# Two graph layers with normalised residuals, 16 sequences on one core: the last tiles' order, the flag's place and the last root are changed

## The chip, the cores and the metric

The kernel runs on one core of one Trainium2 chip. A core has TensorE (PE, matrix products, with its weight loads as PEld), VectorE (DVE), ScalarE (ACT), GpSimd (POOL) and SyncE (SP), each with an instruction queue of its own, and DMA engines that move data between HBM and the on-chip memory. Engines wait for each other by semaphores. The metric is the device time of one execution in microseconds (us); lower is better.

## The reference, cut to what matters

There are 16 sequences of 1024 rows and 256 columns, each with an adjacency matrix of zeros and ones. Layer 0 adds to x a weighted sum of rows, and normalises each row. Layer 1 does so again with other weights:

```python
# layer 0, for adjacency of one kind
alpha = sigmoid(where(adj == 1, leaky((x * a0) @ x.T), -big))
x1 = layernorm(x + alpha @ x + bias)
# layer 1
H = x1 @ W;  s, d = H @ a_src, H @ a_dst
e = where(adj != 0, exp(-leaky(s[:, None] + d[None, :])), 0)
h = (e @ H) / e.sum(-1)
out = layernorm(x1 + elu(h))        # (v - mean) / sqrt(var + 1e-5)
```

The reference allows more kinds of adjacency. The kernel runs a fast pass for one kind and keeps a flag; if the flag says that the input or the numbers don't fit, a general pass (not run with these inputs) follows.

## The kernel before, in words

A sequence is cut into 8 tiles of 128 rows. `one_kind_pass` is a software pipeline written out by hand (`manual_schedule`: each engine takes its instructions in the order in which the program names them). In round b the scores of sequence b (layer 0), the sums of layer 1 of sequence b - 1 (`prev`) and the final scaling and storing of sequence b - 2 (`done`) stand side by side. Sequence 15 is the last. Behind the rounds only its layer 1 is left, and what remains of sequence 14. This stretch, called the end here, begins at L995, and it is what the change rewrites, with a little of the last round ahead of it.

What the steps are:

- `weights(b, m, t0, n)` (L651): VectorE makes the layer 1 weights e for 128 source rows m, here for half of the columns at a time.
- `sum1` (L661): one TensorE product of e with H, 257 columns (256 and the sum of the weights). Eight of them make one tile. `multiply1` (L1042) does the eight of one tile; the first four tiles are done together, one m after the other (L1018 to L1030); the last tile, number 7, is done in two halves of columns by `multiply_halves` (L1051).
- `elu(b, t, ...)` (L692): VectorE inverts the sum of the weights (L698, L699), ScalarE does Relu (L707) and Exp (L708) straight from the product. Tile 6 of the last sequence does the Relu on VectorE (L704, L705).
- `add(b, t)` (L710): VectorE joins both with x1 (L713, L720, for earlier sequences L715) and takes the row's moments (`stats`, L346 and L348). For earlier sequences `deviation1` (L364 on ScalarE) takes them.
- `center` (L388): GpSimd makes from the moments of several tiles the factor 1/sqrt(var + eps) by a power and one Newton step, and mean times factor (L356 to L394: eight small instructions).
- `scale1(b, t)` (L399): ScalarE normalises one tile, 256 columns; `scale0` does the same for x1. `store` (L733) issues a DMA of some tiles on SyncE's queue, in one case on ScalarE's.
- `end_half(c)` (L1072): all of the above for one half of tile 7, with moments into `st_end`.
- `root` and `invert_roots` (L998, L1004): the factors of tiles 6 and 7, with ScalarE's square root, VectorE's reciprocal and one Newton step, then two scalings on VectorE (L1129). The square root needs another function table on ScalarE, whose load shows as L1002.
- `total` (L1092): one small TensorE product sums the flags of 128 partitions; VectorE converts it (L1097), and `values_load` (L1104) has every engine read it into a register. The engines branch on it behind everything else; the last two tiles are stored in the branch that the flag selects (L1477), on SyncE.

In the end of the kernel before, the order is: first four tiles' products; then per tile t the products of tile t + 1 and `elu`, `add` of the tiles behind; the sum of the flag between the products of tiles 5 and 6; its conversion between the sums of tiles 4 and 5; its read on VectorE behind the sum of tile 5, on ScalarE ahead of the scalings of tiles 6 and 7 of sequence 14. GpSimd makes the factors of tiles 0 to 2, then of 3 to 5. PSUM tiles come from three pools, `ps_e`, `ps_t` and `ps_acc`.

## Time and profile before

| what | us |
|---|---|
| median of three runs | 1214.81 (1214.66 to 1215.09) |
| the profiled execution | 1214.68 |
| its span, first to last instruction | 1212.8 |
| VectorE busy | 1005.7 |
| ScalarE busy | 833.6 |
| GpSimd busy | 390.8 |
| last TensorE instruction ends | 1204.45 |
| last store issued (L1477) | 1208.80 |

The span is what the trace shows; the time of the execution lies 1.9 us above it. All starts below are us from the span's start. In the rows of a timeline the first number is the start, the second the duration, then engine, line, operation and what it writes and reads, and in brackets the idle time before it with what ended it. The granted TensorE clock is 0.998 of full speed in this execution.

### The profile page before, as it was taken

What the parts mean: (1) busy time and instruction counts of PE and PEld (TensorE: products, weight loads), DVE (VectorE), ACT (ScalarE), POOL (GpSimd) and SP (SyncE); (2) the same over time, 40 slices, a digit from 0 to 9 for tenths busy, and PEclk for the clock granted to TensorE, in tenths of its full rate; (3) what the DMA queues carried; (4) which work ended last, traced back from release to release, by engine and by line L of the source; (5) the groups of instructions that cost most, each with busy time, mean ns of one, the idle gap of its engine ahead of it and who ended that gap; (6) DMA issues with size and microseconds to landing.
All of it is one profiled execution on the core that took longest, in us unless ns stands there. A gap on an engine that the chain in (4) does not pass through costs nothing.

```text
span 1212.8 us, 16010 instructions
## 1 busy us (share of the span) xinstructions
PE 1203.4 (99%) x4373; PEld 819.0 (68%) x4373; DVE 1005.7 (83%) x1778; ACT 833.6 (69%) x2134; POOL 390.8 (32%) x716
## 2 busy tenths in 40 slices
PE   9999999999999999999999999999999999999997
PEld 7757657576675766758667586775757657576686
DVE  5798896988969789797897978979798897988956
ACT  4574767767677666875768757786676767767674
POOL 2310433504334142432414324143250433404343
PEclk9999999999999999999999999999999999999999
DMA  9768788697887878788697886978869688687412
GB/s 201 143 137 156 131 159 169 132 191 136 143 174 137 182 149 154 156 146 179 137 180 134 153 183 127 182 138 155 174 133 192 124 155 177 131 187 135 114 48 73
DMA packets 611609, 181.98 MB, mean 150 GB/s; under 512 B 488116, under 2 KB 593976, under 8 KB 611512
## 3 DMA queue, kind: packets, MB, share of 16 engines
q1 hardware_dynamic: 589328, 138.21, 57.0%
q0 software_dynamic: 20528, 41.95, 18.7%
q8 instruction: 37, 0.61, 0.2%
q10 hardware_dynamic: 1656, 0.72, 0.2%
q14 instruction: 60, 0.49, 0.2%
HBM read 153.09 MB, written 61.28 MB: 177 GB/s over the span
## 4 chain that ended last, share of the span: by engine, by line
PE 99%; DVE 0%; ACT 0%; issue 0%; ACTq 0%; DVEq 0%
PE acc L662 36%; PE pe L262 20%; PE pH L602 9%; PE pV L497 9%; PE pQ L497 8%; PE pW L497 8%; PE pR L497 4%; PE acc L416 2%; PE busy L149 0%; PE pxT L235 0%; PE pal L333 0%; ACT y L399 0%; ACT y_kept L399 0%; ACT L1002 0%; DVE y L713 0%
## 5 line engine op out<-in xcount | busy, mean ns | idle before, releaser
L662 PE MATMUL acc<-H,e 128*128 128x257 f32 x2032 | 446.9, 380 | 0.0
L662 PEld LDWEIGHTS acc<-H,e 128*128 128x128 f32 x2032 | 385.0, 190 | 69.0 <-issue 13.9
L262 PE MATMUL pe<-xa,xT 128*128 128x384 f32 (+1 forms) x720 | 249.2, 486 | 0.0
L262 PEld LDWEIGHTS pe<-xa,xT 128*128 128x128 f32 x720 | 133.9, 190 | 91.4 <-issue 52.9
L657 DVE SCALAR_TENSOR_TENSOR e<-p,pq_kept,adj 128x1024 f32<-128x1024 f32 (+1 forms) x136 | 159.9, 1229 | 0.1
L292 POOL TENSOR_TENSOR al<-ident,al 128x128 f32<-128x128 f32 x128 | 109.1, 865 | 140.6 <-DVE al L278 140.5
L475 DVE TENSOR_TENSOR al<-al 128x1024 f32<-128x1024 f32 (+2 forms) x105 | 143.8, 1369 | 5.1
L272 DVE TENSOR_TENSOR tb<-tb,low 128x384 f32<-128x384 f32 (+1 forms) x180 | 105.9, 596 | 46.2 <-ACT low L271 44.6
L130 ACT ACTIVATE junk<-adj,minus 128x2048 bf16<-128x2048 bf16 x64 | 127.3, 1990 | 0.1
L270 ACT ACTIVATE tb<-pe 128x384 f32<-128x384 f32 (+1 forms) x180 | 88.1, 489 | 56.1 <-PE pe L262 34.8
L104 POOL CAST adj<-x 128x1 bf16<-128x1 f32 x15 | 3.4, 223 | 352.4 <-DMA x<-y_rows 222.5
L602 PE MATMUL pH<-Wx,yT 128*128 128x258 f32 x480 | 114.1, 380 | 0.0
L497 PE MATMUL pV<-al,S 128*128 128x512 f32 x240 | 108.4, 593 | 0.0
L602 PEld LDWEIGHTS pH<-Wx,yT 128*128 128x128 f32 x480 | 91.1, 190 | 25.3 <-issue 6.7
L497 PE MATMUL pW<-al,x 128*128 128x512 f32 x240 | 107.9, 592 | 0.0
L497 PE MATMUL pQ<-al,x 128*128 128x512 f32 x240 | 107.9, 592 | 0.0
L325 DVE SCALAR_TENSOR_TENSOR al<-al,adj 128x512 f32<-128x512 f32 (+3 forms) x153 | 83.8, 564 | 17.5 <-DMA al<-mir 17.5
L707 ACT ACTIVATE h<-acc,rinv 128x256 f32<-128x256 f32 x81 | 38.1, 470 | 85.3 <-DVE rinv L699 75.7
L688 ACT ACTIVATE sums<-acc,tiny 128x1 f32<-128x1 f32 x45 | 11.8, 261 | 123.3 <-PE acc L662 123.3
L271 ACT ACTIVATE low<-pe 128x512 f32<-128x512 f32 (+1 forms) x192 | 94.9, 494 | 0.0
L278 DVE SCALAR_TENSOR_TENSOR al<-tb,adj 128x1024 f32<-128x1024 f32 (+3 forms) x120 | 90.9, 758 | 4.5
L399 ACT ACTIVATE y_kept<-y_kept,mr,r 128x256 f32<-128x256 f32 x120 | 64.9, 588 | 29.0 <-POOL mr L394 27.8
(152 smaller groups left out, 1661.6 us busy)
## 6 DMA issues: line engine op xcount, KB each, us to landing
adj<-in_adjT POOLq DMA_DIRECT2D x30, 1024.0 KB, 8.3
x<-in_x SPq DMA_DIRECT2D x15, 1024.0 KB
y_rows<-Z SPq DMA_DIRECT2D x240, 64.0 KB
x<-y_rows SPq DMA_DIRECT2D x30, 512.0 KB
out<-y_kept SPq DMA_DIRECT2D x30, 512.0 KB
xT<-in_x SPq DMA_DIRECT2D x112, 128.0 KB
p<-p_row POOLq DMA_DIRECT2D x15, 512.0 KB, 4.1
mir<-tb SPq DMA_DIRECT2D x60, 112.0 KB
```

What stands on the lines that cost most here:

```text
L130: nc.scalar.activation(junk, rows, AF.Square, bias=minus1, scale=2.0, accum_out=chk[:, b * CHECKS + n : b * CHECKS + n + 1],)
L262: nc.tensor.matmul(pe[:, 0:w], lhsT=xTs[b][:, c, ts(jt, P)], rhs=xas[b][:, c, ds(jt * P + o, w)], start=(c == 0), stop=(c == ND - 1),)
L270: nc.scalar.activation(tb[:, ds(o, w)], pe[:, 0:w], AF.Tanh, scale=0.5)
L271: nc.scalar.activation(low[:, 0:w], pe[:, 0:w], AF.Tanh, scale=0.5 * SLOPE)
L272: nc.vector.tensor_tensor(tb[:, ds(o, w)], tb[:, ds(o, w)], low[:, 0:w], ALU.max)
L278: nc.vector.scalar_tensor_tensor(als[b][:, jt, c0:c1], tbs[b, jt][:, c0 - jt * P : c1 - jt * P], 1.0, adjs[b, jt // HT][:, jt % HT, c0:c1] ...
L292: nc.gpsimd.tensor_tensor(diag, ident2, diag, ALU.add)
L475: nc.vector.tensor_tensor(out_, in0, in1, ALU.subtract)
L497: nc.tensor.matmul(banks[bank], lhsT=lhs[:, jt, :], rhs=rhs[:, jt, :], start=first and jt == 0, stop=jt == HT - 1, skip_group_check=True,)
L602: nc.tensor.matmul(pt, lhsT=x1Ts[b][:, c, ts(t, P)], rhs=Wx[:, c, :], start=(c == 0), stop=(c == ND - 1),)
L657: nc.vector.scalar_tensor_tensor(e, p_bcs[b][:, cols], q, rows, ALU.mult, ALU.min)
L662: nc.tensor.matmul(acc, lhsT=es[b][:, m, ts(t, P)], rhs=Hs[b][m], start=(m == 0), stop=(m == NT - 1),)
```

## The change

It touches the last round and the end alone.

- In the last round, the sum of tile 6 of sequence 14 moves ahead of the first four `weights`; the scalings of x1 for tiles 4 to 7 move from the last round into the end, behind the roots of sequence 14. These, with the sum of tile 7 and two deviations, move from step m = 4 to m = 3 of the first products, ahead of `weights` 6. A table set for ScalarE that holds both logarithm and exponential is named there.
- Four scalings of sequence 14 and their store move to right behind the first four tiles' products.
- The flag is summed behind the first four tiles; the products of tiles 4 to 6 are all named ahead of the first `elu`; the flag is converted behind the inverted sums of tiles 0 and 1, and read there, ahead of tile 0's sum.
- GpSimd makes the factors of tiles 0 to 3, of 4 and 5, and of 6 by itself. ScalarE scales two tiles ahead of tile 6's exponential and two behind it, then tile 4 between the halves, 5 behind them, and 6 behind the root. The stores are of tiles 0 to 3, and of 4 and 5, both on SyncE.
- Tile 7's factor is exp(-0.5 ln(var + eps)) on ScalarE with the same Newton step; there is no reciprocal, and VectorE scales tile 7 alone.
- The first half of tile 7 takes its PSUM tile from `ps_t`.

```diff
@@ add @@
-        full = (b, t) == (B - 1, NT - 2)
-        return stats(y, None if full else mv1s[b][:, t, :], f"1_{b}_{t}")
+        return stats(y, mv1s[b][:, t, :], f"1_{b}_{t}")
@@ the last round @@
             if last and t == 7:
+                add(prev, t - 1)
                 for m in range(4):
                     weights(b, m, 0, HT)
...
-            if t >= 1 and (last or t != 6):
+            if t >= 1 and t != (7 if last else 6):
                 add(prev, t - 1)
...
-            if last and t in (5, 7):
+            if last and t == 5:
                 for q in range(HT):
-                    scale0(b, (t - 5) // 2 * HT + q)
+                    scale0(b, q)
@@ the end @@
-    def root(t, st):
-        nc.vector.bn_aggr(mv1s[last][:, t, :], st)
-        r = roots_sb[:, t - (NT - 2) : t - (NT - 2) + 1]
-        nc.scalar.activation(r, mv1s[last][:, t, 1:2], AF.Sqrt, bias=eps)
-    def invert_roots():
-        v, r = mv1s[last][:, NT - 2 :, 1], roots_sb
-        nc.vector.reciprocal(r, r)
-        n = const.tile([P, 2], F32, tag="newton", name="newton")
+    def root():
+        mv = mv1s[last][:, NT - 1, :]
+        nc.vector.bn_aggr(mv, st_end)
+        v, r = mv[:, 1:2], const.tile([P, 1], F32, tag="root", name="root")
+        nc.scalar.activation(r, v, AF.Ln, bias=eps)
+        nc.scalar.activation(r, r, AF.Exp, scale=-0.5)
+        n = const.tile([P, 1], F32, tag="newton", name="newton")
...
     for m in range(NT):
-        if m in (3, 4):
-            weights(last, m + 3, 0, HT)
-        if m == 4:
+        if m == 3:
             add(done, NT - 1)
             for q in (NT - 2, NT - 1):
                 deviation1(done, q)
             r1s[done] = center(mv1s[done], f"1_{done}", unit=1.0 / D)
+            nc.scalar.preload_act_table_set("natural_log_exp_and_others")
+            for q in range(HT, NT):
+                scale0(last, q)
+        if m in (3, 4):
+            weights(last, m + 3, 0, HT)
...
+    for q in range(HT):
+        scale1(done, q)
+    store(done, 0, HT)
     check_pq(last)
...
-            acc = acc1(last, end, *((ps_e, "e") if c else (ps_acc, "acc")))
+            acc = acc1(last, end, *((ps_e, "e") if c else (ps_t, "t")))
...
-    for t in range(end):
-        if n_first - 1 <= t < end - 1:
-            multiply1(t + 1)
-        if t == 5:
-            multiply_halves()
-        if t == 4:
-            total = ps_t.tile([P, HT, P], F32, tag="t", name="total")[0:1, 0, 0:1]
-            nc.tensor.matmul(total, lhsT=any_bad, rhs=ones, start=True, stop=True)
+    total = ps_t.tile([P, HT, P], F32, tag="t", name="total")[0:1, 0, 0:1]
+    nc.tensor.matmul(total, lhsT=any_bad, rhs=ones, start=True, stop=True)
+    for t in range(n_first, end):
+        multiply1(t)
+    elu(last, 0, accs[0])
+    elu(last, 1, accs[1])
+    nc.vector.tensor_copy(flag, total)
+    multiply_halves()
+    n_bad = nc.values_load(
+        flag, min_val=0, max_val=P, skip_runtime_bounds_check_because="a number of partitions"
+    )
+    scale1(done, HT)
+    add(last, 0)
+    for t in range(2, end):
         elu(last, t, accs[t])
-        if 1 <= t < 6:
+        if t < 6:
             add(last, t - 1)
         if t == 5:
-            nc.vector.tensor_copy(flag, total)
             add(last, t)
         if t == 6:
-            st_full = add(last, t, invert)
-        if t in (4, 5):
-            r1s[last] += center(mv1s[last][:, ds(3 * t - 12, 3), :], f"1_{last}_{t}")
-        if t == 5:
-            n_bad = nc.values_load(
-                flag, min_val=0, max_val=P, skip_runtime_bounds_check_because="a number of partitions"
-            )
-        for q in range(2 * t - 4, 2 * t - 2) if 2 <= t < 6 else []:
+            add(last, t, invert)
+        for q in {2: (5, 6), 3: (7,)}.get(t, ()):
             scale1(done, q)
-            if q in (3, 7):
-                store(done, q - 3, HT)
-        if t == 5:
-            for q in range(3):
-                scale1(last, q)
-            store(last, 0, 3)
+        if t == 3:
+            store(done, HT, HT)
+        for t0, n in {4: [(0, 4)], 5: [(4, 2)], 6: [(6, 1)]}.get(t, []):
+            r1s[last] += center(mv1s[last][:, ds(t0, n), :], f"1_{last}_{t0}")
+        for q in {5: (0, 1), 6: (2, 3)}.get(t, ()):
+            scale1(last, q)
+    store(last, 0, HT)
...
     end_half(0)
-    scale1(last, 3)
     scale1(last, 4)
-    store(last, 3, 2)
     end_half(1)
-    root(end, st_end)
-    root(end - 1, st_full)
-    r = invert_roots()
     scale1(last, 5)
-    store(last, 5, 1, nc.scalar)
-    for q in (6, 7):
-        y = ys[last][q]
-        nc.vector.tensor_scalar(
-            y, y, mv1s[last][:, q, 0:1], r[:, q - 6 : q - 5], ALU.subtract, ALU.mult
-        )
+    store(last, 4, 2)
+    r = root()
+    scale1(last, NT - 2)
+    y = ys[last][end]
+    nc.vector.tensor_scalar(y, y, mv1s[last][:, end, 0:1], r, ALU.subtract, ALU.mult)
     return n_bad
```

More of the change, by code (lines that the diff above doesn't have):

```diff
@@ L1013, in invert_roots @@
         return r
-    roots_sb = const.tile([P, 2], F32, tag="root", name="root")
     n_first = 4
```

## The prediction, made before the result was known

> **What bounds the kernel now.** I read the page first: how long each engine is busy, and the chain that ended last.
>
> ```profile
> PE 1203.4 (99%) x4373; PEld 819.0 (68%) x4373; DVE 1005.7 (83%) x1778; ACT 833.6 (69%) x2134; POOL 390.8 (32%) x716
> ...
> PE 99%; DVE 0%; ACT 0%; issue 0%; ACTq 0%; DVEq 0%
> ```
>
> TensorE (PE) is busy for 99% of the span and carries 99% of the chain, so only two things can move the time: TensorE's work, which the change leaves as it is, and the few us in which TensorE no longer sets the end. Where those begin is told by the chain of waits, in order of time, from 1165 us on (start us, us, what).
>
> ```profile
> 1172.50 24.59 PE acc L662 x112
> ...
> 1199.59 1.09 ACT y_kept L399 x2
> 1200.68 1.18 ACT y L399 x3
> ...
> 1202.06 0.46 ACT y_last L708
> ...
> 1204.77 0.26 DVE h_end L1079
> ...
> 1205.44 0.98 ACT L1002
> ...
> 1206.73 0.49 ACT root L1002 x2
> ...
> 1208.36 0.41 DVE y_last L1129
> ```
>
> TensorE runs without a gap from 1172.50 to 1197.09. Then the chain leaves it: for one flag read and five scalings on ScalarE (L399), behind which tile 6's exponential (L708, 1202.06) stands, and from there over VectorE and ScalarE. The products end at 1204.45 (timeline), the last half tile's work starts on VectorE at 1204.68, the table load (L1002) and the two square roots hold the chain from 1205.44 to 1207.22, and the second of two scalings ends it at 1208.77. The timeline gives the single rows (start us, us, engine, line, operation).
>
> ```profile
> 1190.18 0.43 DVE L713 SCALAR_TENSOR_TENSOR y<-y,h 128x256 f32<-128x256 f32 x1 [0.53 <-ACT y L708]
> ...
> 1195.23 0.24 POOL L356 TENSOR_SCALAR ve<-mv 128x3 f32<-128x3 f32 x1 [7.30 <-DVE rinv L698]
> ...
> 1197.97 0.43 POOL L394 TENSOR_SCALAR mr<-mr 128x3 f32<-128x3 f32 x1
> ...
> 1200.93 0.16 DVE L698 TENSOR_SCALAR rinv<-acc 128x1 f32<-128x1 f32 x1 [0.47 <-PE acc L662]
> ...
> 1204.68 0.33 DVE L1079 TENSOR_SCALAR h_end<-acc,rinv_end 128x128 f32<-128x128 f32 x1
> ...
> 1205.44 1.28 ACT L1002 ACT_TABLE_LOAD   x1
> ```
>
> To be seen: tile 0's sum starts at 1190.18; the roots of three tiles on GpSimd (POOL) run from 1195.23 to 1198.40; tile 6's sum of weights is read at 1200.93, when its product has just ended; the table load lasts 1.28 us, and the root follows 0.01 us behind it. How long a read of the flag holds an engine's sequencer stands in the view of the tile flag:
>
> ```profile
> L1104 ACTq TENSOR_LOAD <-flag x1: 467/467/467, 1199.0 to 1199.0; - x1
> L1104 DVEq TENSOR_LOAD <-flag x1: 543/543/543, 1200.3 to 1200.3; - x1
> ...
> L1104 POOLq TENSOR_LOAD <-flag x1: 786/786/786, 1203.3 to 1203.3; - x1
> ```
>
> Last, SyncE's own waits: the final store is not held by its queue.
>
> ```profile
> SPq L1477 <- DVE y_last L1129: 2.9, 1, 2.9
> ```
>
> SyncE had been ready for 2.9 us when VectorE's last scaling released it at 1208.80. From there to the end of the span it is 4.0 us (transfer, branches, closing), which the change leaves alone. So I work out when that scaling ends, and compare with 1208.77.
>
> **Part 1: the order on VectorE ahead of the products.** Tile 6's sum of sequence 14 moves ahead of the first four weights. Its two instructions took 0.79 us (1177.12 to 1177.91), so the first weights go from 1174.24 to 1175.03 and, at 0.68 us, are there at 1175.71. TensorE takes 24.59 us for 112 products, 0.2196 us each, and its 16 products of the tile before end at 1176.01. Cover: 0.30 us; each later one of the weights has more, as TensorE needs 1.76 us per step and VectorE 0.68. If the cover is gone, the whole of it goes on the end. What is moved is the same work in total, so the checks of the flag are summed by 1187.92 as before, 2.2 us ahead of TensorE's end of the first four tiles, 1197.10 less 32 x 0.2196 = 1190.07; the sum of the flag on TensorE therefore doesn't stall it, and its place in the queue costs no more there than at 1197. I cost TensorE at 0.
>
> **Part 2: ScalarE between the products.** Four scalings of x1 (2.07 us) move from 1178.52 behind the deviations, with a table load ahead of them. Tile 7's sum now has two weights fewer ahead of it, 1.35 us, so its deviation ends about 1180.80 (before: 1182.15). Load 1.28 us: 1182.1; scalings: 1184.2; GpSimd's roots for sequence 14 took 5.7 us (1182.24 to 1187.93) and now end about 1186.6; four scalings of sequence 14 follow until 1188.8; tile 0's Relu is due at 1189.32. All of it lies in ScalarE's wait of 7.2 us ahead of that Relu, so it costs 0, with 0.5 us of cover; what is gone beyond it would still hide behind part 3 for 0.9 us. The store of these rows leaves SyncE about 1188.9, while no transfer runs.
>
> The Trainium skill, "ScalarE: Activation LUTs", section "What ACT_TABLE_LOAD costs", adds a drain of about 1.38 us to the load; the row shows none (the root starts 0.01 us after the load), and with a drain the load would still be hidden here, so the sum is the same by either.
>
> **Part 3: the flag ahead of tile 0's sum.** VectorE now converts the flag first. TensorE's sum of it ends about 1190.2, the conversion (0.12 us) at 1190.4, then VectorE reads the flag. That it holds the engine is seen on ScalarE, which went on 0.12 us after its own read. Bounds for VectorE's hold: 0 (it is the sequencer that loads) and 0.79 (POOL's row). I take VectorE's own row, 0.543, with 0.1 behind it: tile 0's sum starts at 1191.05 instead of 1190.18, **0.87 us later**. Waiting behind it on VectorE are the sums of all tiles. They follow at 1.70 us per tile (1191.67 to 1193.37), so tile 3's moments end at 1197.72 instead of 1196.85. The cadence catches up only where VectorE used to wait for products: tile 6's row at 1200.93 had 0.47 us idle ahead of it, and tile 4's 0.27. So tile 6's weights are still read at about 1200.93.
>
> The Trainium skill, "DMA: Bandwidth & Descriptors", section "Latency and other measured facts", has about 600 ns as the floor of a register load, which speaks against reading early; the rows here go down to 0.466 us, and by the page tile 0's sum would be 0.06 us later still.
>
> **Part 4: ScalarE ahead of tile 6's exponential.** The read and two scalings of sequence 14 leave this place. But two scalings of the last sequence stay ahead of the exponential, and they wait for GpSimd's roots of four tiles, which can't start before tile 3's moments: 1197.80. Four columns took 3.33 us (1160.68 to 1164.01) and 3.48 (1156.18 to 1159.66); I take 3.33: 1201.13. Scalings from 1201.25, exponential at 1202.25: **0.19 us later** than 1202.06. Two more scalings behind it push the last tile's Relu to 1203.60 (before 1203.35), so VectorE's chain for the halves is 0.25 us late: the second half starts at 1204.93, the last moments are there at 1206.57.
>
> **Part 5: the root.** No load now stands ahead of it, so the logarithm starts 0.1 us after the moments, at 1206.68 (the root of before: 1206.73). Logarithm and exponential of 128x1 have no row together; the nearest are the roots with the same operands, 0.278 and 0.294 us, and the dependent pairs of L612 and L613, 0.29 us from start to start. Ends: 0.48 for both (the two roots) and 0.94 (two of 256 columns, 0.47); I take 0.29 + 0.28: 1207.25. The reciprocal goes (0.195); three Newton steps of 0.195 each begin at 1207.29; the one scaling runs from 1207.88 to 1208.29, as tile 6's goes to ScalarE. That one needs GpSimd's root of one column, about 1206.7 by an estimate from the rows (2.05 us for 8 columns of the power, 1.04 for 4, 0.89 for 3), and ScalarE at 1207.2; it ends about 1207.75, beside the Newton steps, with 0.5 us of cover. Stores of tiles 4 and 5 leave at 1205.65 and take 0.75 us of transfer, clear of the last one.
>
> **Sum.** +0.25 (late halves), -0.30 (no wait for the load), +0.08 (logarithm and exponential against two roots), -0.19 (reciprocal), -0.33 (one scaling fewer; 1208.03 to 1208.36): -0.49, about **-0.5 us**. The profiled execution took 1214.68, a span of 1212.8 and 1.9 around it; it becomes 1214.2. The median of the runs shown, 1214.81, lies 0.13 above it, so I forecast 1214.3. About 0.2% (2.4 us) is what a measurement of this kernel can tell from no change; my sum is a fifth of that.
>
> **Rivals.**
> A, **the products set the end again**: if VectorE's hold is near 0, or GpSimd's roots of four are 0.75 us shorter, the exponential starts at 1201.39, right behind tile 6's weights. The second half then starts at 1204.50, as early as its product allows, and the last scaling ends at 1207.85: -0.9 us, 1213.9. For it: a load runs on the sequencer. Against it: ScalarE visibly stood still for its read. This is also the most that the change can give, since TensorE's end stays.
> B, **the read takes the place of the stall, and the kernel is slower**: every 0.1 us by which the flag delays tile 0's sum goes through tile 3's moments, GpSimd and ScalarE's two scalings to the end, one for one. It decides from a hold of about 1.0 us on (0.54 + 0.49); at 1.5 us it is +0.5, 1215.3. For it: the read waits for a value that the same engine wrote just before, of which no row exists, and POOL's row has 0.79. Against it: 1.0 is above all five rows of the read.
> C, **the first weights come late**: part 1's cover of 0.30 us is gone, TensorE stalls once, and all of it is paid: with 0.8 us of stall +0.3, 1215.1.
> D, **the change doesn't do what it says**: a second table load comes back ahead of the logarithm. The program of the changed kernel holds one load in this stage, so I give it no share.
>
> **How the numbers follow.** Forecast 0.61, A 0.14, B 0.10, C 0.08, a cause that I don't name 0.07. The range runs from A, with 0.5 below for the medians' scatter (1214.66 to 1215.09) and for unknown rows, to B at 1.5 us of hold: 1213.4 to 1215.4. Slower by over 0.2%: 0.02 of B, 0.01 of C, 0.02 unnamed, 0.05. Faster by over 0.2%: 0.03, unnamed alone, since A ends at -0.9. Within: 0.92.
>
> **What would show it.** Tile 0's sum near 1191.05 (part 3); the roots of tiles 0 to 3 on GpSimd ending near 1201.1 and ScalarE waiting for them (part 4); the products ending at 1204.45 as before, with no gap near 1176 and 1190 (part 1); the table load near 1181 inside ScalarE's wait (part 2); the logarithm 0.1 us behind the moments, one scaling of 0.41 us, the final store issued near 1208.3 (part 5). Wrong would be a gap on TensorE, ScalarE idle for more than 0.3 us behind the last moments, or a span that moves by over 1 us either way.

## The result and the profile after

| | before | after |
|---|---|---|
| median of 18 runs each, us | 1214.53 (1213.91 to 1215.09) | 1216.84 (1216.22 to 1218.30) |
| profiled execution, us | 1214.68 | 1216.43 |
| its span, us | 1212.8 | 1214.6 |

The ratio after to before is 1.002, with a 95% interval of 1.0012 to 1.0027. The changed kernel is 2.3 us slower; I had forecast 1214.3, about 0.5 us faster, with a range up to 1215.4. So both the sign and the range were wrong.

The page of the changed kernel, the same two lines as shown of before: busy time of TensorE first, then the chain by engine.

```profile
PE 1202.9 (99%) x4373; PEld 818.6 (67%) x4373; DVE 1005.2 (83%) x1776; ACT 834.4 (69%) x2135; POOL 394.0 (32%) x724
...
PE 96%; DVE 2%; DMA 1%; SPq 0%; ACT 0%; POOL 0%; issue 0%; DVEq 0%
```

TensorE is busy for the same time to 0.5 us, but the chain now leaves it earlier. The chain of waits of the changed kernel shows where (start us, us, what):

```profile
1172.21 17.62 PE acc L662 x80
...
1190.17 1.15 DVEq L1095
...
1191.42 0.44 DVE y L713
...
1201.27 0.25 POOL mr L394
...
1201.54 1.09 ACT y L399 x2
1202.63 0.37 ACT y_last L708
...
1206.61 0.22 DVE mv L1001
...
1206.86 0.30 ACT root L1003
...
1207.18 0.21 ACT root L1004
...
1208.00 0.41 DVE y_last L1127
```

It leaves TensorE at 1189.96, behind the sum of the flag (before: 1197.09). From there VectorE's sequencer (DVEq) holds it for 1.15 us with the read of the flag, then the sums of the tiles, GpSimd's roots of four (ending 1201.51), two scalings, tile 6's exponential. The last moments are there at 1206.82, logarithm and exponential follow, one scaling ends at 1208.41. In before that last scaling ended at 1208.77. By this view alone the changed kernel would be faster. The chain view ends with the last *counted* instruction, though: branches, semaphores and drains are not in it.

The view of the tile flag of the changed kernel (ns min/median/max, then first and last start):

```profile
L1095 ACTq TENSOR_LOAD <-flag x1: 1097/1097/1097, 1190.2 to 1190.2; - x1
...
L1095 DVEq TENSOR_LOAD <-flag x1: 1154/1154/1154, 1190.2 to 1190.2; - x1
L1095 PEldq TENSOR_LOAD <-flag x1: 492/492/492, 1202.0 to 1202.0; - x1
```

The read held VectorE for 1.154 us where I had taken 0.543. TensorE's read, 12 us later, took 0.492. The timeline of the changed kernel gives the rows that answer to those of before, and the stores:

```profile
1180.54 1.28 ACT L1020 ACT_TABLE_LOAD   x1
...
1181.84 2.08 ACT L399 ACTIVATE x<-x,mr,r 128x256 f32<-128x256 f32 x4
...
1189.21 7.55 SPq L734 DMA_DIRECT2D out<-y_kept  x2
...
1191.42 0.43 DVE L713 SCALAR_TENSOR_TENSOR y<-y,h 128x256 f32<-128x256 f32 x1 [1.29 <-ACT y L708]
...
1206.93 0.24 POOL L394 TENSOR_SCALAR mr<-mr 128x1 f32<-128x1 f32 x1
...
1208.50 0.37 SPq L1473 DMA_DIRECT2D out<-y_last  x1
```

Tile 0's sum stands at 1191.42. The table load lies near 1181 and the scalings follow 0.02 us behind it. The first half of sequence 14 is stored from 1189.21, 1.0 us ahead of the read. GpSimd's last instruction, tile 6's mean times factor, stands at 1206.93, and the final store is issued at 1208.50, 0.30 us earlier than in before.

So the work ends earlier and the span ends later: from the final store's issue to the span's end it is 6.1 us (1214.6 less 1208.50), in before 4.0. What lies there is seen in the instructions of the lines of the last branch. First the line of the branch, in the changed kernel (only GpSimd's sequencer, POOLq, is copied):

```profile
L1469 POOLq EVENT_SEMAPHORE  x5: 17/43/43, 1210.3 to 1210.7; - x5
...
L1469 POOLq COMPARE_BRANCH  x1: 45/45/45, 1206.9 to 1206.9; - x1
...
L1469 POOLq INC_SWDGE_SEM  x1: 732/732/732, 1210.8 to 1210.8; - x1
```

and the closing line behind it, also in the changed kernel:

```profile
L1507 POOLq EVENT_SEMAPHORE  x4: 17/17/17, 1213.8 to 1214.5; - x4
L1507 POOLq DRAIN  x3: 46/107/2273, 1211.5 to 1214.4; - x3
```

GpSimd's sequencer takes the branch at 1206.9, as it issues its last computing instruction. Its next instruction is at 1210.3: 3.4 us with nothing. Then come five semaphores, an INC_SWDGE_SEM of 0.73 us at 1210.8, and a DRAIN of 2.27 us from 1211.5 to 1213.8. 0.8 us later the program ends. What an engine does from its branch on is called its closing here. The same in the kernel before, the branch:

```profile
L1473 POOLq EVENT_SEMAPHORE  x5: 17/43/43, 1206.9 to 1207.2; - x5
...
L1473 POOLq COMPARE_BRANCH  x1: 45/45/45, 1204.2 to 1204.2; - x1
...
L1473 POOLq INC_SWDGE_SEM  x1: 732/732/732, 1207.3 to 1207.3; - x1
```

and its closing line:

```profile
L1511 POOLq EVENT_SEMAPHORE  x4: 17/17/17, 1212.0 to 1212.7; - x4
L1511 POOLq DRAIN  x3: 46/107/2273, 1208.0 to 1212.5; - x3
```

There the branch is at 1204.2, the long drain runs from 1208.0 to 1210.3, and GpSimd's next instruction is at 1212.0: GpSimd waited 1.7 us for the others, so its closing cost nothing. In the changed kernel the others wait for it. SyncE's waits in the changed kernel agree:

```profile
SPq L1507 <- DMA p_row<-pT: 2.0, 1, 2.0
...
SPq L1473 <- DVE y_last L1127: 1.1, 1, 1.1
```

SyncE stands 2.0 us for a semaphore of GpSimd's queue of DMAs (p_row<-pT was issued in the rounds; INC_SWDGE_SEM sets it at 1211.4), and had been ready 1.1 us before the final store could be issued.

My theory after this (C): GpSimd's factor of tile 6 moved its branch 2.7 us later (from 1204.2 to 1206.9), and a closing of 6 to 7 us behind it now sets the end. Two rivals: the read's hold makes it slower (R), or the order and size of the stores does (S).

### The profile page after: what moved, and what is told of

It reads as the page before. It is cut to its first block, busy times and chain, and to the rows that moved or that the text cites. A ratio compares the mean times of both kernels' runs of the same rounds, so it can differ in the third digit from the quotient of the medians.

```text
span 1214.6 us, 16018 instructions
## 1 busy us (share of the span) xinstructions
PE 1202.9 (99%) x4373; PEld 818.6 (67%) x4373; DVE 1005.2 (83%) x1776; ACT 834.4 (69%) x2135; POOL 394.0 (32%) x724
## 4 chain that ended last, share of the span: by engine, by line
PE 96%; DVE 2%; DMA 1%; SPq 0%; ACT 0%; POOL 0%; issue 0%; DVEq 0%
PE acc L662 36%; PE pe L262 20%; PE pH L602 9%; PE pW L497 8%; PE pV L497 8%; PE pQ L497 8%; PE pR L497 4%; PE acc L416 2%; DMA al<-mir 1%; SPq L302 0%; PE busy L149 0%; DMA mir<-tb 0%; PE pxT L235 0%; PE pal L333 0%; DVE al L278 0%
```

## The experiments

All times below are relative to the end of the products on TensorE, in the profiled execution of each kernel, so that kernels can be laid beside each other. "Drain" is the end of GpSimd's long DRAIN, "time" the median less that of before in the same session of runs (interval of the ratio).

| kernel | tile 0's sum | last moments end | final store issued | GpSimd's branch | drain | span end | time |
|---|---|---|---|---|---|---|---|
| before | -14.27 | 1.87 | 4.35 | -0.26 | 5.87 | 8.37 | |
| after | -12.74 | 2.66 | 4.34 | 2.73 | 9.64 | 10.48 | +2.31 (1.0012 to 1.0027) |
| e1 | -12.75 | 2.66 | 4.61 | -0.07 | 6.33 | 8.76 | +0.63 (0.9997 to 1.0015) |
| e2 | -14.26 | 1.84 | 4.32 | 0.34 | 6.58 | 8.47 | +0.05 (0.9991 to 1.0009) |
| e3 | -14.26 | 1.84 | 4.33 | 1.89 | 7.94 | 8.81 | +0.48 (0.9995 to 1.0013) |
| e4 | -14.26 | 1.88 | 4.36 | 3.69 | 10.15 | 10.98 | +2.54 (1.0011 to 1.0030) |
| e12 | -14.27 | 1.87 | 4.16 | 2.21 | 8.58 | 9.42 | +1.10 (0.9999 to 1.0017) |
| e5 | -13.35 | 2.08 | 4.03 | -0.66 | 5.72 | 8.39 | -0.10 (0.9994 to 1.0012) |
| e6 | -14.26 | 2.05 | 4.00 | -0.11 | 6.92 | 8.32 | +0.47 (0.9994 to 1.0012) |
| e9 | -14.26 | 1.87 | 3.86 | -0.25 | 5.88 | 8.43 | -0.25 (0.9989 to 1.0007) |
| e10 | -14.26 | 1.84 | 4.93 | -0.28 | 5.86 | 8.75 | +0.64 (0.9995 to 1.0013) |
| e11 | -14.26 | 1.84 | 3.74 | -0.31 | 6.02 | 8.37 | -0.46 (0.9986 to 1.0004) |
| e7 | -13.87 | 1.99 | 3.94 | -0.17 | 6.85 | 8.47 | +0.30, one run |
| e13 | -12.59 | 2.81 | 4.76 | 0.65 | 7.71 | 8.68 | +0.14, one run |
| e8 | -13.35 | 1.72 | 3.84 | -0.71 | 5.75 | 8.79 | -0.18 (0.9992 to 1.0010) |

**e1: tile 6's factor taken off GpSimd.** The changed kernel, with logarithm, exponential and Newton step over two columns, and VectorE scaling tiles 6 and 7. The read stays where the change put it.

```diff
-        v, r = mv[:, 1:2], const.tile([P, 1], F32, tag="root", name="root")
+        v, r = mv1s[last][:, NT - 2 :, 1], const.tile([P, 2], F32, tag="root", name="root")
...
-        for t0, n in {4: [(0, 4)], 5: [(4, 2)], 6: [(6, 1)]}.get(t, []):
+        for t0, n in {4: [(0, 4)], 5: [(4, 2)]}.get(t, []):
...
-    scale1(last, NT - 2)
-    y = ys[last][end]
-    nc.vector.tensor_scalar(y, y, mv1s[last][:, end, 0:1], r, ALU.subtract, ALU.mult)
+    for q in (6, 7):
+        y = ys[last][q]
+        nc.vector.tensor_scalar(
+            y, y, mv1s[last][:, q, 0:1], r[:, q - 6 : q - 5], ALU.subtract, ALU.mult
+        )
```

> The changed kernel, but tile 6's factor is made together with tile 7's by logarithm and exponential on two columns, and VectorE scales both; GpSimd makes no factor of tile 6. Theory C (closing): in the profile of the changed kernel GpSimd issues its branch at 1206.88, goes on at 1210.33, sets the semaphores of its DMA queue (0.73 us) and drains (2.27 us) until 1213.85, and the program ends 0.75 us behind that; in the kernel before its branch is at 1204.2, the drain ends at 1210.31 and GpSimd waits until 1212.03. So 7.0 us from GpSimd's last instruction to the end of its drain set the end. With its last factors made about 1204.4 the drain ends at 1211.2, the end is set by the last store again, one scaling (0.33 us) later than in the changed kernel: about 1.8 us faster than the changed kernel, within 0.3 us of the kernel before. Theory R (the flag's read, 1.15 us in front of tile 0's sum, is what was lost): no faster than the changed kernel, 2.3 us over the kernel before. Theory S (the last store lands late behind the larger stores on its queue): as R.

Measured 1215.15 beside 1214.52. Everything up to the last moments is as in the changed kernel, to 0.01 us; the final store even leaves 0.27 us later; and the kernel is 1.7 us faster than the changed one (+0.63 against +2.31, from two sessions whose kernel before has the same median, 1214.52 and 1214.53; nine of its eleven runs lie below the fastest of the changed kernel's, 1216.22). The branch line of this kernel:

```profile
L1470 POOLq EVENT_SEMAPHORE  x5: 17/43/43, 1207.2 to 1207.6; - x5
...
L1470 POOLq COMPARE_BRANCH  x1: 45/45/45, 1204.3 to 1204.3; - x1
...
L1470 POOLq INC_SWDGE_SEM  x1: 732/732/732, 1207.6 to 1207.6; - x1
```

The branch is 2.6 us earlier than in the changed kernel (1204.3 against 1206.9), and the closing lies in cover again. Theory C stands; the read and the stores, which are the same in both, can't be the main cause.

**e2, e3, e4: a dose on the kernel before.** Nothing of the change, only a copy of 128x1 on GpSimd whose result nobody reads, waiting for the first half's moments, for tile 7's moments, or for the inverted roots. One line, in three places (where the tile `late` is made is left out):

```diff
     end_half(1)
+    nc.gpsimd.tensor_copy(late, st_end[:, 0, 1:2])            # e2
     root(end, st_end)
+    nc.gpsimd.tensor_copy(late, mv1s[last][:, end, 0:1])      # e3
     root(end - 1, st_full)
     r = invert_roots()
+    nc.gpsimd.tensor_copy(late, r[:, 0:1])                    # e4
```

> The kernel before with one more copy of 128x1 on GpSimd that nothing reads, released by the moments of tile 7's first half, about 1204.9. Theory C: GpSimd's branch at about 1204.9, its drain ends at 1211.9, just short of 1212.03 when the others are ready: 0 to +0.2 us. Theories R and S: 0.

> The kernel before with the same copy, released by tile 7's moments, about 1206.4. Theory C: branch at 1206.5, drain until 1213.5, +1.4 us over the kernel before, though nothing waits for the copy. Theories R and S: 0.

> The kernel before with the same copy, released by the finished roots, about 1208.0. Theory C: branch at 1208.1, drain until 1215.1, +3.1 us over the kernel before. Theories R and S: 0.

Measured 1214.57, 1215.00 and 1217.06 beside 1214.52. The final store is issued within 0.03 us of that of before in all three. An idle copy of 0.35 us therefore costs 2.5 us if it is placed late enough. The branch line of e4, and behind it its closing line:

```profile
L1475 POOLq EVENT_SEMAPHORE  x5: 17/42/43, 1212.5 to 1212.8; - x5
...
L1475 POOLq COMPARE_BRANCH  x1: 45/45/45, 1209.5 to 1209.5; - x1
```

```profile
L1513 POOLq EVENT_SEMAPHORE  x4: 17/17/17, 1216.0 to 1216.7; - x4
L1513 POOLq DRAIN  x3: 46/107/2273, 1213.7 to 1216.5; - x3
```

e3 and e4 cost less than expected (+0.48 for +1.4, +2.54 for +3.1): the next instruction came 2.6 and 3.0 us behind the branch, and the closing took 6.05 and 6.46 us in place of the 7.0 I had allowed. Over all runs, branch to end of the drain took 6.05 to 7.06 us, of which the step from the branch to the next instruction is the part that varies (2.6 to 3.6).

**e12: tile 6's factor alone, on the kernel before.** GpSimd makes it, ScalarE scales the tile; the square root, the flag and the order stay.

```diff
-            st_full = add(last, t, invert)
+            add(last, t, invert)
+            r1s[last] += center(mv1s[last][:, ds(t, 1), :], f"1_{last}_{t}")
...
-    root(end - 1, st_full)
...
-    for q in (6, 7):
-        y = ys[last][q]
-        nc.vector.tensor_scalar(
-            y, y, mv1s[last][:, q, 0:1], r[:, q - 6 : q - 5], ALU.subtract, ALU.mult
-        )
+    scale1(last, end - 1)
+    y = ys[last][end]
+    nc.vector.tensor_scalar(y, y, mv1s[last][:, end, 0:1], r, ALU.subtract, ALU.mult)
```

> The kernel before with one part of the change alone: tile 6's factor on GpSimd by itself and its scaling on ScalarE; tile 7's by square root as before. Theory C: GpSimd has its flag read until 1204.1, then eight instructions of one column (2.4 us), so its branch comes about 1206.6, 2.1 us behind the products' end; 6.1 to 7.0 us to the end of its drain and 0.8 from there: +0.5 to +1.5 us against the kernel before, although VectorE's last scaling goes and the last store is issued 0.3 us earlier. Theory R (the flag's read is what was lost): 0.3 us faster, as the flag is read where it was.

Measured 1215.70 beside 1214.60, +1.10, though the store is issued 0.19 us earlier. The closing line of this kernel:

```profile
L1508 POOLq EVENT_SEMAPHORE  x4: 17/17/17, 1213.7 to 1214.4; - x4
L1508 POOLq DRAIN  x3: 46/107/2273, 1211.4 to 1214.2; - x3
```

The drain ends at 1213.7 and the span at 1214.5. In the four kernels whose drain ends latest (after, e3, e4, e12) the span ends 0.83 to 0.87 us behind it; in e13 0.97, in all others 1.4 to 3.0. Before's span end, 8.37, less 0.85 gives 7.5 as the point up to which the drain is covered. What lies beyond it is 0.4, 1.1, 2.1 and 2.6 us for e3, e12, after and e4; their medians rose by 0.48, 1.10, 2.31 and 2.54. Only the last two stand clear of no change by their intervals, but the four lie on one line, and the size of the slowdown is on it.

**e5: e1, and the first store of sequence 14 behind the read.** This asks why the read took twice its time: the store under way (T), or four engines reading at once (Q).

```diff
     for q in range(HT):
         scale1(done, q)
-    store(done, 0, HT)
     check_pq(last)
...
+    store(done, 0, HT)
     scale1(done, HT)
     add(last, 0)
```

> e1_root6_off_gpsimd with one more edit: the store of sequence 14's tiles 0 to 3 is issued behind the flag's read, not 1 us ahead of it. In e1 the four reads at 1190.4 took 1.05 to 1.14 us; in the kernel before those without a transfer under way took 0.47 to 0.54, those with one 0.79. Theory T (traffic): the read lengthens while a store is under way; now 0.46 to 0.55 us, tile 0's sum 0.6 us earlier, the end about 0.5 us earlier than e1, that is 0 to +0.2 us against the kernel before. Theory Q (four engines read the same word at once): the reads stay at 1.05 to 1.15 and the time stays e1's, +0.6.

Measured 1214.46 beside 1214.56. The view of the tile flag in this kernel:

```profile
L1093 SPq TENSOR_LOAD <-flag x1: 462/462/462, 1190.3 to 1190.3; - x1
L1093 ACTq TENSOR_LOAD <-flag x1: 463/463/463, 1190.3 to 1190.3; - x1
...
L1093 DVEq TENSOR_LOAD <-flag x1: 542/542/542, 1190.3 to 1190.3; - x1
```

Still four engines read at the same time, and each takes 0.46 to 0.54 us. So Q falls as the cause by itself, and the store's traffic is needed. Tile 0's sum is 0.6 us earlier than in e1, and the final store 0.58.

**e7 and e13: one reader under the store's traffic.** The kernel before has a read beside as much traffic: GpSimd's of 0.786 us. The DMA view of that stretch of before, 1203.33 to 1204.12 (queue, packets, MB, share of the 16 DMA engines), and then the one of the reads in the changed kernel, 1190.17 to 1191.33:

```profile
q1 hardware_dynamic: 269, 0.28, 96.9%
```

```profile
q1 hardware_dynamic: 392, 0.40, 94.3%
```

One reader took 0.79 us at a share of 97%, four took 1.06 to 1.15 at 94%. Do four readers add to it under traffic (TQ), or not (T)? Both kernels are e1 with VectorE alone reading early, and all engines again at tile 5; in e13 the early value is used, to pick a column of the tile `spare`, which is zeroed ahead of the flag's conversion.

```diff
-    n_bad = nc.values_load(
-        flag, min_val=0, max_val=P, skip_runtime_bounds_check_because="a number of partitions"
-    )
+    early = nc.values_load(
+        flag, [mybir.EngineType.DVE], min_val=0, max_val=P, skip_runtime_bounds_check_because="a number of partitions"
+    )
+    nc.vector.tensor_copy(late, spare[:, ds(early, 1)])      # e13 alone
...
+        if t == 5:
+            n_bad = nc.values_load(
+                flag, min_val=0, max_val=P, skip_runtime_bounds_check_because="a number of partitions"
+            )
```

> This is e1 with one reader at the early place: only VectorE reads the flag there, 1.0 us behind the issue of the 512 KB store, and all engines read it again at tile 5. It asks what makes the difference between GpSimd's read in the kernel before, 0.786 us with the DMA engines 97% busy, and the four reads of 1.05 to 1.15 us in the changed kernel with them 94% busy. If traffic alone sets it (T), VectorE's early read stays at 1.1 us (1.0 to 1.2) with the store under way, and tile 0's sum stays 12.75 us ahead of the end of the products. If four readers at once add to it under traffic (TQ), it is about 0.8 us (0.75 to 0.9), and tile 0's sum comes some 0.3 us earlier. If readers alone set it (Q), it is 0.54; the run with the store behind the read speaks against that. The final store hangs on two scalings on VectorE as in e1, so it would be issued 4.6 us behind the products under T and about 4.3 under TQ; the time is one look and decides nothing.

> The question of the run before (one reader under the store's traffic), with a use for the early value, so that the read stays in the program: VectorE takes a column of a zeroed tile at the value's place, into a tile that nobody reads. Else as before: e1, with all engines reading again at tile 5. If traffic alone sets the length (T), VectorE's early read takes 1.1 us (1.0 to 1.2). If four readers at once add to it under traffic (TQ), it takes about 0.8 us (0.75 to 0.9), like GpSimd's single read in the kernel before with the DMA engines 97% busy. If it is 0.54, readers at once alone set it (Q), against the run with the store behind the read. The time is one look and decides nothing; the added copy and zeroing cost VectorE some 0.2 to 0.4 us ahead of tile 0's sum.

e7 says nothing of the question: nothing used the early value, and its trace holds no early read (tile 0's sum at -13.87). The view of the tile flag in e13:

```profile
L1097 DVEq TENSOR_LOAD <-flag x1: 1155/1155/1155, 1190.7 to 1190.7; - x1
L1118 SPq TENSOR_LOAD <-flag x1: 472/472/472, 1197.5 to 1197.5; - x1
L1118 ACTq TENSOR_LOAD <-flag x1: 464/464/464, 1199.1 to 1199.1; - x1
L1118 DVEq TENSOR_LOAD <-flag x1: 320/320/320, 1201.7 to 1201.7; - x1
```

A single reader, 1.0 us behind the issue of the same store, takes 1.155 us, as among four. TQ falls: readers at once add nothing. Of T only half is shown. The store is needed (e5), but the share of the DMA engines doesn't set the length. In e13 itself, ScalarE's read at 1199.14 falls into the last half microsecond of the second store of sequence 14, whose share over this read is

```profile
q1 hardware_dynamic: 132, 0.12, 76.3%
```

and it takes 0.464 us, as without a transfer. In the kernel before, TensorE's read stands in the middle of the stores and takes as long as GpSimd's:

```profile
L1104 PEldq TENSOR_LOAD <-flag x1: 790/790/790, 1202.3 to 1202.3; - x1
```

The reads of over 1 us all begin within 0.25 us of a store's first transfer. TensorE's began 0.7 us behind one and GpSimd's 1.7, in an unbroken run of transfers. Whether it is the time since the transfers began, or what else differs there, no run separates.

**e6: e1, with the conversion and the read back at tile 5.**

```diff
-    nc.vector.tensor_copy(flag, total)
     multiply_halves()
-    n_bad = nc.values_load(
-        flag, min_val=0, max_val=P, skip_runtime_bounds_check_because="a number of partitions"
-    )
...
         if t == 5:
+            nc.vector.tensor_copy(flag, total)
             add(last, t)
...
+        if t == 5:
+            n_bad = nc.values_load(
+                flag, min_val=0, max_val=P, skip_runtime_bounds_check_because="a number of partitions"
+            )
```

> e1_root6_off_gpsimd with the flag's conversion and read back at tile 5, as in the kernel before; its sum on TensorE stays behind the first four tiles. If the early read costs what part 3 of the prediction said and more (1.3 us on tile 0's sum), then tile 0's sum starts at 1190.2 again, GpSimd's factors of four tiles end about 1200.0, tile 6's exponential is no longer held by them, and the end comes 0.5 to 0.8 us earlier than in e1: -0.1 to +0.1 us against the kernel before. If the early read is no loss (theory of the change), the time is e1's or above.

Measured 1215.03 beside 1214.56. In the profile it does what it should: tile 0's sum is where before has it, the store leaves at 4.00 and the span ends at 8.32. The time, +0.47 with an interval from -0.7 to +1.5 us, neither confirms nor refutes that.

**e9: the kernel before with logarithm and exponential, and nothing else.**

```diff
             r1s[done] = center(mv1s[done], f"1_{done}", unit=1.0 / D)
+            nc.scalar.preload_act_table_set("natural_log_exp_and_others")
...
-        nc.scalar.activation(r, mv1s[last][:, t, 1:2], AF.Sqrt, bias=eps)
...
-        nc.vector.reciprocal(r, r)
+        nc.scalar.activation(r, v, AF.Ln, bias=eps)
+        nc.scalar.activation(r, r, AF.Exp, scale=-0.5)
```

> The kernel before with the root alone changed: logarithm and exponential on the two columns of tiles 6 and 7, the table named behind the roots of sequence 14, no square root and no reciprocal. By part 5 of the prediction: -0.30 (no wait for the load) +0.08 -0.19, about -0.4 us. If theory C is all there is to the end, that is what the time shows, since GpSimd's last instruction stays at 1203.6 and the last store sets the end. If another engine's closing sets the end, 0.

Measured 1214.31 beside 1214.56. The store is issued 0.49 us earlier, as the parts say, and the median is 0.25 lower; the interval includes no change. In the profile the span ends no earlier (8.43 against 8.37); the next two runs show why.

**e10, e11: the final store alone.** Three dependent VectorE operations more behind the Newton step, or no Newton step for tiles 6 and 7 (that step of the computation is left out).

```diff
         nc.vector.scalar_tensor_tensor(r, n, 1.5, r, ALU.add, ALU.mult)
+        for _ in range(3):                                     # e10
+            nc.vector.tensor_scalar(r, r, 1.0, None, ALU.mult)
...
-        n = const.tile([P, 2], F32, tag="newton", name="newton")            # e11
-        nc.vector.scalar_tensor_tensor(n, v, EPS, r, ALU.add, ALU.mult)
-        nc.vector.scalar_tensor_tensor(n, n, -0.5, r, ALU.mult, ALU.mult)
-        nc.vector.scalar_tensor_tensor(r, n, 1.5, r, ALU.add, ALU.mult)
```

> The kernel before with three more dependent instructions of VectorE (a multiplication of the two roots by 1) ahead of the last scalings: the last store is issued 0.58 us later. If the last store sets the end: +0.6. If SyncE's closing (it waits once for each of some 20 semaphores, and fetches the code of the closing) sets the end with room to spare: less, down to 0.

> The kernel before without the Newton step of tiles 6 and 7 (left out, three instructions of VectorE): the last store is issued 0.6 us earlier. If the last store sets the end: -0.6. If the closing of the other engines sets it, as e9 suggests (store 0.49 us earlier, end at the same place): -0.1 to 0.

Store +0.58 gave +0.64, store -0.61 gave -0.46. Each interval includes no change, but in the same session every run of e10 (from 1214.63) lies above every run of e11 (up to 1214.52). The profiled executions show less: the span ends 0.38 us later in e10, and not earlier in e11 (8.37). The semaphore records of the traces tell what SyncE waits for behind the final store. Tile 5's store of 128 KB, on ScalarE's queue, has landed at 5.62 us behind the products in before, 5.89 in e9, 5.83 in e11, and SyncE goes on at 5.64, 5.91 and 5.84. The final store lands at 6.68, 6.59 and 6.53, and holds SyncE for another 0.3 us in before, but not in e9 and e11. So even while GpSimd's closing is covered, the tail doesn't hang on the final store alone, as I had assumed: later, it costs; earlier, SyncE still waits for the other transfer. What made e11's median lower stays open; the end of the products alone differs by up to 1.9 us between the profiled executions (1203.89 in e3, 1205.80 in e4).

**e8: the best that these parts suggest.** e5, with tile 6's logarithm and exponential made ahead of tile 7's moments, its Newton step in VectorE's wait for tile 7's exponential, tile 6 scaled by ScalarE, and GpSimd's factors in two groups of three.

```diff
-        for t0, n in {4: [(0, 4)], 5: [(4, 2)]}.get(t, []):
+        for t0, n in {3: [(0, 3)], 5: [(3, 3)]}.get(t, []):
...
     end_half(1)
-    scale1(last, 5)
-    store(last, 4, 2)
-    r = root()
+    guess(end - 1)
+    scale1(last, 4)
+    nc.vector.bn_aggr(mv1s[last][:, end, :], st_end)
+    guess(end)
+    r = newton(end - 1)
...
+    scale1(last, 5)
+    store(last, 3, 3)
+    scale(ys[last][end - 1], r, mr)
+    r = newton(end)
```

(`guess` is the logarithm and exponential of one tile, `newton` its Newton step.)

> A version made from what was found: e5, and the factors of tiles 0 to 2 and 3 to 5 on GpSimd as in the kernel before, tile 6's factor by logarithm and exponential ahead of tile 7's, with its Newton step in VectorE's wait for tile 7's, tile 6 scaled by ScalarE. GpSimd's last instruction about 1204, so its closing ends at 1211; tile 6's exponential follows its weights (about 1201.4), the products set the end again, and one scaling is left on VectorE: 0.6 to 1.0 us faster than the kernel before under theory C; under Q, 0.3 us less of that.

Measured 1214.38 beside 1214.56: the gain didn't come. The timeline of this kernel at the end:

```profile
1206.93 0.59 ACT L399 ACTIVATE y_last<-y_last,mr_end,root 128x256 f32<-128x256 f32 x1
...
1207.15 0.41 DVE L1136 TENSOR_SCALAR y_last<-y_last,mv,root 128x256 f32<-128x256 f32 x1
1208.09 0.93 SPq L1482 DMA_DIRECT2D out<-y_last  x1
```

ScalarE's scaling of tile 6 ends at 1207.52 and VectorE's of tile 7 at 1207.56, 3.31 behind the products; but the store is issued only at 1208.09, and its issue takes 0.93 us where other kernels show 0.37. SyncE was late for it: the store of tiles 3 to 5, which this version issues at 1207.05, takes until 1207.42, SyncE's branch follows at 1207.47, and its next instruction 0.46 us behind that. From the final store's issue to the end it is 4.95 us, and the semaphore records show two transfers in it: SyncE goes on 0.01 us after the store of tiles 3 to 5 has landed (6.35 us behind the products), and again after the final one has (7.01). In all kernels whose GpSimd closing is covered, this stretch took 3.8 to 5.0 us (4.02 in before). No version that I ran is shown to beat the kernel before.

## Why the prediction was wrong, point by point

**The failed step** is the sentence on SyncE's wait: "From there to the end of the span it is 4.0 us (transfer, branches, closing), which the change leaves alone." It took the tail as one number that hangs on the final store. It hangs on the last of several closings, and part 5 put new instructions on GpSimd ahead of one of them. Part 5 asked of GpSimd's root of tile 6 only whether the scaling on ScalarE would have it in time (it did: 1207.17, the scaling at 1207.29). It did not ask what comes behind it on GpSimd. The lines of the kernel before, shown above, held the answer: drain to 1210.3, next instruction at 1212.0, so 1.7 us of cover. GpSimd's last instruction there ended at 1203.63 and its flag read at 1204.12, with the branch at 1204.2; by my own estimate its root of tile 6 was to end at 1206.7, which puts the branch 2.2 to 2.5 us later (in the changed kernel it came 0.3 us ahead of that end). Less 1.7, that is a span 0.5 to 0.8 us longer, not 0.5 shorter. Relative to the products the span became 2.1 us longer. The rest is in two sizes: the branch came 3.0 us later (the hold again, through tile 3's moments, behind which GpSimd's factors run back to back from 1198.17 to 1207.17), and the closing took 6.91 us in place of 6.13; 3.0 + 0.8 - 1.7 is the 2.1.

- **What bounds the kernel:** right as far as the counted work goes, TensorE's busy time and end didn't move. The chain's end was taken for the program's end; that was the error above.
- **Part 1 (order on VectorE, 0):** right. The first weights start at 1174.71 and no gap appears on TensorE near 1176 or 1190; the products end at 1204.16, 0.29 us earlier than in before's execution.
- **Part 2 (ScalarE, 0):** right. Load 1180.54 to 1181.82, scalings to 1183.92, GpSimd's roots to 1187.08, sequence 14's scalings to 1189.19. The cover of 0.5 us was used up, since GpSimd's roots ended 0.5 us later than I had worked out: tile 0's Relu (1189.09) came right behind the scalings, 0.06 us late relative to the products, and that hid behind part 3, as I had allowed. The page "ScalarE: Activation LUTs" of the Trainium skill, section "What ACT_TABLE_LOAD costs", adds a drain of about 1.38 us per switch; the next instruction stands 0.02 us behind the load, so this case shows none.
- **Part 3 (the read):** the mechanism was right and the size was off. The mis-sized term is the hold, 0.543 + 0.1, upper bound 0.79: it was 1.154 with 0.10 behind it (ScalarE's row of before has 0.09 behind its read, not the 0.12 that I gave). I took VectorE's row, a read with no transfer beside it, and did not see that my own part 2 had put a store of 512 KB 1.0 us ahead of the read; the upper bound, GpSimd's row, was one with traffic, and even it was too low. Tile 0's sum came 1.53 us late relative to the products, not 0.87. The "DMA: Bandwidth & Descriptors" page of the Trainium skill, section "Latency and other measured facts", has about 600 ns as the floor of a register load; the runs show 0.32 to 0.55 without a transfer, and up to 1.16 beside a store, so the floor lies lower, and what mattered here was not the floor.
- **Part 4 (+0.19, then +0.25):** the path was right, tile 3's moments, GpSimd, two scalings, exponential; with the longer hold it was +0.77 at the exponential and +0.79 at the last moments. GpSimd's roots of four took 3.34 us (taken: 3.33).
- **Part 5 (root and one scaling):** sizes right. Logarithm 0.03 us behind the moments, 0.32 us on to the exponential, which took 0.20 (taken: 0.29 + 0.28); Newton 0.58 up to the scaling's start; one scaling 0.41. From the moments to the end of VectorE it was 1.60 us, in before 2.45.
- **The sum:** forecast -0.49 at the final scaling. It came out as -0.06 (4.26 against 4.32 behind the products), because of the hold. With the read made short (e5), it is -0.32, with one scaling more on VectorE than the change has.
- **Rivals:** B, the read in place of the stall, happened and took the gain, as its mechanism says; my "1.0 is above all five rows of the read" was no reason against it. But it was not what made the kernel slower: e1 keeps the read and loses most of the slowdown. A, C and D did not happen. The cause that decided was among the 0.07 that I didn't name.
- **What would show it:** I listed a span that moves by more than 1 us as a sign of error; it moved by 1.8. The signs I listed for single steps were nearly all met (roots 1201.51 for 1201.1, store 1208.50 for 1208.3): a list of signs that ends at the last computed result can't see what lies behind it.

## What to carry to other kernels

The end of a kernel is the last of all engines' ends, each with a closing of its own: before moving work to an engine late, read from the trace where its last branch and drain stand and how long it waits for the others, since that wait is the whole allowance (1.7 us here, for an engine that is busy 32% of the time). The chain of waits and the timeline stop at computing instructions; the instructions listed under the last branch's line show what follows. A register read's time is to be taken from a row that stands as the new place does, with the same store as far under way: the same DMA share was not enough (0.46, 0.79 and 1.15 us at 76 to 100%). Look at which store is issued in the microsecond ahead of its new place.

## What the runs showed of the hardware

- GpSimd's way out of this kernel: branch to next instruction 2.6 to 3.6 us, INC_SWDGE_SEM 0.73 us, DRAIN 2.27 us (the last two the same in all runs), 6.05 to 7.06 from the branch to the end of the drain. The other engines pay for the branch as well: TensorE's sequencer has its branch at 3.36 us in the changed kernel and 3.78 in before, and VectorE's goes on 3.2 us behind its own. In the changed kernel's gap on GpSimd the DMA view shows four transfers of 8 KB on an instruction queue; for which engine they were, it doesn't say. "Runtime: NRT & Kernel Launch" in the Trainium skill, section "Instruction fetch mechanics", says that a taken branch to a target outside the loaded pages waits for a fetch by DMA. That fits the gap, but no run here moved the branch's target, so it is argued, not shown.
- A register load took 0.46 to 0.55 us with no transfer under way, on any engine and with four at once (e5), in one case 0.32 (VectorE's second read in e13); 0.79 in the middle and the last part of a run of stores (TensorE and GpSimd, before); 1.05 to 1.16 in the first microsecond of a 512 KB store, with one reader (e13) as with four; and 0.464 in the last half microsecond of one, with the DMA engines 76% busy (ScalarE, e13).
- SyncE's closing in this kernel waits for more stores than the final one, and for one on ScalarE's queue too: with the final store issued 0.5 to 0.6 us earlier (e9, e11), SyncE went on 0.01 to 0.02 us behind the landing of tile 5's store, and the span of the profiled execution ended no earlier.
